# Padded rows of pieces and a new order of work at the layer ends of a four-layer graph network

## The chip, the cores and the metric

The kernel runs on one core of one Trainium2 chip. The metric is device time in microseconds (us), the median of several runs. TensorE (PE; its weight loads are PEld), VectorE (DVE), ScalarE (ACT), GpSimd (POOL) and SyncE (SP) have instruction streams of their own and meet through semaphores. SP and POOL also issue DMAs, in the order of their streams.

## What is computed

A graph of N = 3327 nodes with 512 features passes through four layers. `adj` is a dense 0/1 matrix. Layers 0, 1 and 2 are graph attention with 8, 4 and 8 heads, layer 3 is a mean over neighbours with dense weights:

```python
# layers 0, 1, 2  (layer 1 adds self loops to the mask)
h  = max(layernorm(x), 0)
Wh = h @ W                                   # per head
e  = leaky_relu(s1[i] + s2[j], slope 0.2)    # s1, s2: Wh times two vectors
x  = x + elu(softmax(where(adj, e, -inf)) @ Wh)
# layer 3
h  = max(layernorm(x), 0)
agg = (adj @ h) / max(degree, 1)
x  = x + max(concat(h @ W_self + b_self, agg @ W_nb + b_nb) @ W_comb + b_comb, 0)
```

## The kernel before, in words

Nodes are cut into 26 tiles of 128 (the last has 127). Targets go in 7 chunks of four tiles (the last has two, tiles 24 and 25); sources in five groups of 6, 6, 6, 4 and 4 tiles (`JG`, line 67).

**Attention without exponentials per edge.** exp(leaky_relu(s1 + s2)) is one product of node terms where s1 + s2 > 0 and another where it isn't. So for each head and source tile there is a gate (s1 > -s2, by ACT at L550 or DVE at L547), which is ANDed with the mask (L556) and, for the other half, XORed back (L560). Masks and gates are FP8 and are the stationary operand. The moving operand is the node's value terms for both cases. To keep f32 precision each is cut into three bf16 **pieces**: a head's row holds for each case (a "half") 3 x 65 = 195 columns in layers 0 and 2. L588 multiplies the first half with one gate, L591 the second half with the other. In layer 1 the heads are wider: L584 (3 x 129 = 387 bf16 columns) for group 0, and for the other groups f32 pairs (L581) with gates cast up by ACT or DVE (L493).

**Layout of a row** (`dims`, line 102): the first half takes `AO` = 196 columns (195 and a column of ones that gives the degree in layer 0), the row `HW` = 2 x 196 - 1 = 391 columns, 782 bytes. `pieces` (line 298) makes the rows of one tile and stores them to scratch memory `abd`; `load_pieces` (line 498) loads one group of one head, `nj` rows side by side in each partition, into a tile `ab` with seven buffers. Each pass takes two target tiles k; for each source j it runs L588 and L591 for the first k, then for the second. R (L606) sums the pieces.

**Node terms of the next layer, in hooks.** When a chunk is done, its tiles go through stages that `hooks.run` spreads among the passes that follow: s0 `finish` (load own terms `xt`, ELU on ACT and DVE, add on POOL at L664, store) and `norm` (statistics on DVE at L282 and L284, the power on POOL L285 to L287, ACT L289); s1 transposes on PE (L134) with a copy by ACT (L138); s2 projection on PE (L340; in layer 3 L377) and, in layers 0 to 2, the making and storing of pieces; s3 transposes and stores the row scores s1 (`send_s1`, L392 to L395), which the next layer loads as `s1b` (L518). The last chunk has nothing behind it, so its two tiles go through the stages after the layer's last products.

**The end of a layer** (lines 637 to 641): start the first of the last tiles, run what is `left` (in layer 2: own-term projections for layer 3 of the tiles from 22 on, L377 with a bias addition at L380), drain the hooks, then `close()`, then run what is left again. `close` calls `fuse_weights` in layers 0 and 1: it multiplies W_self or W_nb by its half of W_comb in four blocks: load (L170), transpose (L134 on `xt`), four products (L174), copy (L176), store (L177); and one row for the biases (L180, L181).

**Order.** The program is written in one order; a list scheduler then places instructions on their engines by priority, where `after(a, b)` asks that a stand behind b on its engine. `gone` holds the last product of each pass. Each engine then runs its stream strictly in order.

Of the kernel before, what the change touches and what calls it, by code (L numbers as in the profile page):

```python
# [37 lines left out]
P = 128  # L38
# [14 lines left out]
def tile_gnn(ctx: ExitStack, tc: tile.TileContext, x, adj, W0, a01, W1, al, ar, W2, a2,  # L53
# [41 lines left out]

    xs = [x] + [[dram.tile([n * P, D], F32, name=f"x{l}_{c}") for c, (_, n) in enumerate(chunks)]
# [5 lines left out]
    def dims(l):  # L102

        H = heads[l]
        DA = D // H + 1
        AO = 3 * DA + 1
        return H, DA, AO, (2 * AO - 1 if l != 1 else 2 * AO)
# [39 lines left out]
    gone = []  # L147

# [12 lines left out]
    def fuse_weights(i, wc):  # L161
        w_src, b_src = ((Ws, bs), (Wn, bn))[i]
        b = pre.tile([P, KC], F32, name="bv", bufs=1)
        if i == 0:
            nc.gpsimd.dma_start(bias, bc.partition_broadcast(P))
        with nc.allow_non_contiguous_dma(reason="512 values"):
            nc.gpsimd.dma_start(b, b_src.rearrange("(c p) -> p c", p=P))
        for k in range(KC):
            w = pre.tile([P, D], F32, name="xt")
            nc.gpsimd.dma_start(w, w_src[k * P:(k + 1) * P, :])  # L170
            wT = transposed(w, pre, "hT")
            pw = ps.tile([P, D], F32, name="mm")
            for m in range(KC):
                nc.tensor.matmul(pw, wT[:, m, :], wc[:, m, :], start=(m == 0), stop=(m == KC - 1))  # L174
            xo = pre.tile([P, D], F32, name="h")
            nc.scalar.copy(xo, pw)  # L176
            nc.gpsimd.dma_start(Xd[i][k * P:(k + 1) * P, :], xo)  # L177
        pb = ps.tile([P, D], F32, name="mm")
        for m in range(KC):
            nc.tensor.matmul(pb, b[:, m:m + 1].to_broadcast([P, P]), wc[:, m, :], start=(m == 0), stop=(m == KC - 1))  # L180
        nc.vector.tensor_add(bias, bias, pb)  # L181
# [54 lines left out]
    def open_layer(l):  # L236
        L = Layer()
        L.l = l
        if l == 3:
# [40 lines left out]
    def norm(xt, pool):  # L280
# [3 lines left out]
        nc.vector.bn_aggr(mv[:, 0:2], st)  # L284
# [13 lines left out]
    def pieces(L, t, AB, pool, first):  # L298
# [9 lines left out]
        nc.gpsimd.memset(pt[:, :, :, o, 3 * DA:AO] if l == 1 else pt[:, :, o, 3 * DA:AO], 1.0)  # L308
# [14 lines left out]
        if o == two - 1 and l == 1:  # L323
            for a in range(2):
                nc.sync.dma_start(abd[l][g][:, a, :, js, :].rearrange("h p j w -> p h j w"), pt[:, :, a])
        elif o == two - 1:
            stored[t] = nc.sync.dma_start(abd[l][g][:, :, js, :].rearrange("h p j w -> p h j w"), pt).ins.name

    def project(L, t, hT, pool, first):
# [7 lines left out]
        for f in range(2):  # L337
            pw = (accs if first else ps).tile([P, D // 2 + H], F32, name="acc" if first else "mm")
            for k in range(KC):
                nc.tensor.matmul(pw, hT[:, k, :], L.w[:, k, f, :], start=(k == 0), stop=(k == KC - 1))  # L340
# [13 lines left out]
        if l == 1 and KIND[g] != "b":  # L354
            for f in range(2):
# [5 lines left out]
                nc.sync.dma_start(abd[l][g][hs, :, :, jj, :].rearrange("h a p w -> p h a w"),  # L361
                                  pt.rearrange("p h a s d -> p h a (s d)").bitcast(F32))
# [7 lines left out]
    def project_last(L, t, hT, i):  # L370
# [5 lines left out]
        for k in range(KC):  # L376
            nc.tensor.matmul(pw, hT[:, k, :], L.w[i][:, k, :], start=(k == 0), stop=(k == KC - 1))  # L377
        if i == 0:
            y = pre.tile([P, D], F32, name="AB", bufs=1)
            nc.vector.tensor_add(y, pw, bias)  # L380
            nc.sync.dma_start(y1d[c][kk * P:kk * P + n, :], y[:n])
# [7 lines left out]
    def send_s1(L, t, pool, first):  # L389
# [5 lines left out]
        nc.sync.dma_start(s1d[L.l][:, t * P:(t + 1) * P], s1t[:H])  # L395

    def node_stages(L, t, get_x, pool, first=False):
# [7 lines left out]
        def s1():  # L405
            behind = gone[-1] if gone else None
            q["hT"] = transposed(q["h"], mp, "A", 6, behind) if late else transposed(q["h"], pool, "hT", 2, behind)
# [7 lines left out]
        def s3():  # L415
            if L.l != 3:
                send_s1(L, t, pool, first)
# [834 lines left out]
```

## Time and profile before

| | us |
|---|---|
| median of 3 runs | 3674.61 (3668.65 to 3675.11) |
| profiled execution | 3671.68 |
| its span, first to last instruction | 3669.8 |

Stages of the span, from windows of the trace:

| stage | from, to (us) | PE busy | DVE busy | ACT busy | granted PE clock | DMA share |
|---|---|---|---|---|---|---|
| first node terms | 0, 177 | 127.75 | 128.87 | 108.09 | 0.97 | 0.75 |
| layer 0 | 177, 1263 | 1065.72 | 896.78 | 850.46 | 0.99 | 0.73 |
| end of layer 0 | 1263, 1308 | 34.48 | 25.01 | 37.22 | 0.89 | 0.68 |
| layer 1 | 1308, 2156 | 816.41 | 717.92 | 680.43 | 0.99 | 0.78 |
| end of layer 1 | 2156, 2200 | 23.56 | 24.89 | 25.56 | 0.73 | 0.57 |
| layer 2 | 2200, 3309 | 1105.47 | 785.14 | 750.79 | 1.00 | 0.55 |
| end of layer 2 | 3309, 3356 | 37.54 | 10.96 | 10.98 | 0.89 | 0.72 |
| layer 3 | 3356, 3670 | 297.74 | 61.78 | 54.42 | 0.98 | 0.32 |

A busy time counts every moment in which some instruction of the engine is under way. PE's instructions overlap, so its busy time does not tell how fast one follows another; the start times do. The granted clock is the share of TensorE's full clock in the stretch. "Idle before, releaser" behind a group is the time its engine stood still just before it and what ended that.

### The profile page before, as it was taken

How to read it: one execution, taken by the hardware profiler on the slowest of the kernel's cores; microseconds unless marked ns; L12 is line 12 of the kernel's file. 1: busy time of each engine (PE TensorE's matmuls, PEld its weight loads, DVE VectorE, ACT ScalarE, POOL GpSimd, SP SyncE). 2: the span in 40 equal slices, each digit the busy share in tenths (PEclk: the TensorE clock that was granted, in tenths of full speed). 3: DMA queues.
4: the chain of work that ended last, by engine and by line, in shares of the span. 5: the costliest groups of instructions: out<-in, count | busy, mean ns of one | idle time of the engine just before them, and what ended most of it. 6: DMA issues, size and time to landing. Idle time of an engine off the chain costs nothing. (4 is left out here: it accounts for less than half of the span.)

```text
span 3669.8 us, 78902 instructions
## 1 busy us (share of the span) xinstructions
PE 3508.7 (96%) x31348; PEld 3172.0 (86%) x31348; DVE 2651.4 (72%) x5230; ACT 2518.0 (69%) x4170; POOL 589.2 (16%) x832
## 2 busy tenths in 40 slices
PE   7799999999999899999999979999999999998998
PEld 5599999999999778888888859989898989886886
DVE  7698888888887789888888766767776767672121
ACT  5678787777787779888888656767666767571111
POOL 6501221202010102122223220001010101010000
PEclk9999999999999999999999989999999999999999
DMA  7777677777756877777877876545455554476331
GB/s 210 230 207 226 201 226 212 215 220 224 220 189 215 270 262 262 270 257 249 275 249 261 320 229 188 187 169 189 167 182 167 191 171 171 160 276 238 113 104 51
DMA packets 321402, 773.05 MB, mean 211 GB/s; under 512 B 36037, under 2 KB 143560, under 8 KB 320384
## 3 DMA queue, kind: packets, MB, share of 16 engines
q1 hardware_dynamic: 293920, 707.23, 57.6%
q0 software_dynamic: 27104, 60.69, 6.8%
q8 instruction: 249, 4.08, 0.4%
q14 instruction: 129, 1.06, 0.1%
HBM read 661.25 MB, written 128.68 MB: 215 GB/s over the span
## 5 line engine op out<-in xcount | busy, mean ns | idle before, releaser
L588 PE MATMUL acc<-ab,tht 128*128 128x195 bf16 (+1 forms) x10816 | 1872.8, 248 | 20.9 <-DVE tht L556 14.5
L591 PE MATMUL acc<-ab,gt 128*128 128x195 bf16 (+1 forms) x10816 | 1872.3, 249 | 3.1 <-DVE gt L560 2.3
L550 ACT ACTIVATE gt<-s1b,ks 128x512 fp8e4<-128x512 f32 (+1 forms) x2464 | 1456.5, 677 | 279.0 <-issue 150.4
L588 PEld LDWEIGHTS <-tht 128*128 128x128 fp8e4 x10816 | 1060.0, 98 | 28.0 <-DVE tht L556 15.4
L591 PEld LDWEIGHTS <-gt 128*128 128x128 fp8e4 x10816 | 1052.6, 97 | 26.6 <-issue 14.6
L581 PE MATMUL acc<-ab,t 128*128 128x258 f32 x4160 | 544.6, 289 | 22.7 <-ACT t L493 19.6
L581 PEld LDWEIGHTS acc<-ab,t 128*128 128x128 f32 x4160 | 520.2, 192 | 35.8 <-ACT t L493 23.1
L556 DVE TENSOR_TENSOR tht<-gt,m 128x768 uint32<-128x768 uint32 (+3 forms) x560 | 447.8, 800 | 141.6 <-ACT gt L550 138.8
L560 DVE TENSOR_TENSOR gt<-tht,m 128x768 uint32<-128x768 uint32 (+3 forms) x560 | 447.0, 799 | 8.2
L493 ACT CAST t<-tht 128x1536 fp32r<-128x1536 fp8e4 x208 | 300.7, 1469 | 57.6 <-PE acc L581 47.2
L547 DVE TENSOR_SCALAR gt<-s1b,ns 128x512 fp8e4<-128x512 f32 (+1 forms) x448 | 213.9, 480 | 150.0 <-PE acc L591 138.3
L664 POOL TENSOR_TENSOR xt<-xt,e 128x512 f32<-128x512 f32 x78 | 114.7, 1471 | 1270.8 <-DVE e L663 1230.6
L788 PE MATMUL acc<-y,mf 128*128 128x512 f32 x1352 | 309.8, 391 | 1.3 <-DVE mf L783 1.3
L550 ACT ACTIVATE tht<-s1b,ks 128x512 fp8e4<-128x512 f32 (+1 forms) x504 | 306.9, 679 | 2.0 <-DMA s1b<-s 2.0
L788 PEld LDWEIGHTS acc<-y,mf 128*128 128x128 f32 x1352 | 253.6, 188 | 57.4 <-DVE mf L783 1.7
L606 DVE TENSOR_REDUCE R<-acc 128x130 f32<-128x390 f32 x416 | 214.7, 555 | 81.8 <-PE acc L591 81.7
L584 PE MATMUL acc<-ab,tht 128*128 128x387 bf16 x1248 | 225.5, 329 | 4.6 <-DMA ab<-ab 2.5
L785 ACT CAST mf<-m 128x768 fp32r<-128x768 fp8e4 (+1 forms) x78 | 59.1, 762 | 244.7 <-PE acc L788 232.9
L340 PE MATMUL mm<-w,hT 128*128 128x260 f32 (+1 forms) x832 | 200.3, 393 | 13.2 <-ACT hT L138 10.4
L340 PEld LDWEIGHTS mm<-w,hT 128*128 128x128 f32 x832 | 156.9, 194 | 38.4 <-ACT hT L138 11.2
L584 PEld LDWEIGHTS <-tht 128*128 128x128 fp8e4 x1248 | 118.7, 98 | 81.9 <-DMA ab<-ab 2.9
L319 POOL TENSOR_TENSOR pt<-r 128x520 bf16<-128x520 f32 (+1 forms) x116 | 143.2, 1254 | 266.1 <-DVE r L315 249.3
(132 smaller groups left out, 3138.2 us busy)
## 6 DMA issues: line engine op xcount, KB each, us to landing
ab<-ab SPq DMA_DIRECT2D x336, 586.5 KB
ab<-ab SPq DMA_DIRECT2D x224, 391.0 KB
ab<-ab SPq DMA_DIRECT2D x112, 774.0 KB
ab<-ab SPq DMA_DIRECT2D x112, 516.0 KB
ab<-ab SPq DMA_DIRECT2D x56, 582.0 KB
s1b<-s SPq DMA_DIRECT2D x120, 256.0 KB
m<-mask SPq DMA_DIRECT2D x72, 384.0 KB
ab<-pt SPq DMA_DIRECT2D x40, 516.0 KB
```

The lines of the kernel that those rows point to most:

```text
L340: nc.tensor.matmul(pw, hT[:, k, :], L.w[:, k, f, :], start=(k == 0), stop=(k == KC - 1))
L493: (nc.scalar.copy if KIND[g] == "s" else nc.vector.tensor_copy)(t[:, :k1 - k0, :nj], th[a][g][:, k0:k1])
L547: nc.vector.tensor_scalar(gv[:, :, jj, :], s1v, L.ns2[:, j, h:h + 1], 2.0, op0=ALU.is_gt, op1=ALU.mult, saturate=False)
L550: nc.scalar.activation(gv[:, :, jj, :], s1v, AF.Relu, bias=L.ks2[:, j, h:h + 1], scale=BIG, saturate=False)
L556: nc.vector.tensor_tensor(pu, gu, mu, ALU.bitwise_and)
L560: nc.vector.tensor_tensor(gu, pu, mu, ALU.bitwise_xor)
L581: mm = nc.tensor.matmul(acc[k][:, :2 * DA], thr[g][:, k - ks[0], jj, :], ab[a][g][:, jj, :], start=(j == 0), stop=(j == NT - 1), skip_grou ...
L584: mm = nc.tensor.matmul(acc[k][:, :3 * DA], th[a][g][:, k, jj, :], ab[a][g][:, jj, :3 * DA], start=(j == 0), stop=(j == NT - 1), skip_grou ...
L588: nc.tensor.matmul(acc[k][:, :3 * DA + o], th[0][g][:, k, jj, :], ab[0][g][:, jj, :3 * DA + o], start=(j == 0), stop=False, skip_group_che ...
L591: mm = nc.tensor.matmul(acc[k][:, AO - o:HW], th[1][g][:, k, jj, :], ab[0][g][:, jj, AO - o:HW], start=False, stop=(j == NT - 1), skip_gro ...
L606: nc.vector.tensor_reduce(R[:, k], v.rearrange("p a (s d) -> p a d s", s=3), AX.X, ALU.add)
L788: nc.tensor.matmul(acc[k], mf[:, jj, :], y2[g][:, jj, s, :], start=(j0 + jj == 0 and s == 0), stop=(j0 + jj == NT - 1 and s == 1))
```

## The change

It has four parts.

1. **Rows.** In layers 0 and 2 each half is rounded up to 200 columns and the row is 400 (800 bytes). The columns 195 to 199 of both halves are set to ones, and the degree is the sum of two columns. Layer 1's rows stay. The tile `ab` grows accordingly.
2. **Blocks of weights.** `fuse_weights` becomes the class `Fusion`: loads of biases and of blocks 0 and 1 are issued ahead of the last head, blocks 0 and 1 and the biases are run right behind the last products, and blocks 2 and 3 at the end. Own terms x of the last chunk's tiles are loaded ahead of the last head too, by POOL.
3. **End of layer 2.** The projections that are left are run behind the last products; their bias additions and stores are asked to stand behind the statistics of the last chunk's first tile.
4. **Queues.** Behind the first layer's own node terms, stores of pieces are held back to stage s3 (`to_store`), and row scores are stored by POOL instead of SP. The transposes of tile 25 stand behind the projection of tile 24. Buffers: "A" from 6, 5, 6 to 8, 6, 8 in the three layers, "tht" in layer 1 from 12 to 11, "R" in layer 2 smaller.

The core of the diff:

```diff
+    A_BUFS = [8, 6, 8]
...
         DA = D // H + 1
-        AO = 3 * DA + 1
-        return H, DA, AO, (2 * AO - 1 if l != 1 else 2 * AO)
+        AO = -(-(3 * DA + 1) // 8) * 8 if l != 1 else 3 * DA + 1
+        return H, DA, AO, 2 * AO
...
-        nc.gpsimd.memset(pt[:, :, :, o, 3 * DA:AO] if l == 1 else pt[:, :, o, 3 * DA:AO], 1.0)
+        nc.gpsimd.memset(pt[:, :, :, o, 3 * DA:AO] if l == 1 else
+                         pt[:, :, o].rearrange("p h (a w) -> p h a w", a=2)[..., 3 * DA:AO], 1.0)
...
+    class Fusion:
...
+        def load(self, k, behind):
+            self.w[k] = pre.tile([P, D], F32, name="xt")
+            after(nc.gpsimd.dma_start(self.w[k], self.w_src[k * P:(k + 1) * P, :]), behind)
+
+        def block(self, k, behind):
+            w = self.w.pop(k)
+            wT = transposed(w, pre, "hT", 2, behind)
             pw = ps.tile([P, D], F32, name="mm")
             for m in range(KC):
+                nc.tensor.matmul(pw, wT[:, m, :], self.wc[:, m, :], start=(m == 0), stop=(m == KC - 1))
+            nc.scalar.copy(w, pw)
+            nc.gpsimd.dma_start(Xd[self.i][k * P:(k + 1) * P, :], w)
...
+        def biases(self, behind):
+            pb = ps.tile([P, D], F32, name="mm")
+            for m in range(KC):
+                mm = nc.tensor.matmul(pb, self.b[:, m:m + 1].to_broadcast([P, P]), self.wc[:, m, :],
+                                      start=(m == 0), stop=(m == KC - 1))
+                if m == 0:
+                    after(mm, behind)
+            nc.vector.tensor_add(bias, bias, pb)
...
         if i == 0:
-            y = pre.tile([P, D], F32, name="AB", bufs=1)
-            nc.vector.tensor_add(y, pw, bias)
-            nc.sync.dma_start(y1d[c][kk * P:kk * P + n, :], y[:n])
+            def add():
+                y = pre.tile([P, D], F32, name="AB", bufs=1)
+                sm = nc.vector.tensor_add(y, pw, bias)
+                if behind:
+                    after(sm, stats[-chunks[-1][1]])
+                nc.sync.dma_start(y1d[c][kk * P:kk * P + n, :], y[:n])
+            if behind:
+                return add
+            add()
...
-        nc.sync.dma_start(s1d[L.l][:, t * P:(t + 1) * P], s1t[:H])
+        (nc.sync if first else nc.gpsimd).dma_start(s1d[L.l][:, t * P:(t + 1) * P], s1t[:H])
...
-            behind = gone[-1] if gone else None
+            behind = (L.mm if t == NT - 1 and not first else gone[-1]) if gone else None
...
         def s3():
             if L.l != 3:
+                for to, pt in L.to_store:
+                    nc.sync.dma_start(to, pt)
+                L.to_store = []
                 send_s1(L, t, pool, first)
             elif late:
-                left.append(lambda: project_last(L, t, q["hT"], 0))
+                left.append(lambda: project_last(L, t, q["hT"], 0, gone[-1]))
...
             for h in range(H):
+                if last and h == H - 1:
+                    for k in range(nt):
+                        x_last[t0 + k] = load_x(l, t0 + k, mp, "A", A_BUFS[l], behind=gone[-1])
+                    fusion = close()
+                    if fusion:
+                        fusion.load_biases()
+                        fusion.load(0, gone[-1])
+                        fusion.load(1, gone[-1])
...
-                                    mm = nc.tensor.matmul(acc[k][:, AO - o:HW], th[1][g][:, k, jj, :],
-                                                     ab[0][g][:, jj, AO - o:HW], start=False, stop=(j == NT - 1),
+                                    mm = nc.tensor.matmul(acc[k][:, AO:AO + 3 * DA + o], th[1][g][:, k, jj, :],
+                                                     ab[0][g][:, jj, AO:AO + 3 * DA + o], start=False, stop=(j == NT - 1),
...
-                                nc.vector.tensor_copy(deg2[:n, t0 + k:t0 + k + 1], acc[k][:n, 3 * DA:AO])
+                                nc.vector.tensor_reduce(deg2[:n, t0 + k:t0 + k + 1],
+                                                        acc[k][:n, 3 * DA:AO + 3 * DA + 1:AO], AX.X, ALU.add)
...
         hooks.run(1, 0, 0)
-        run_left()
+        fusion = close()
+        if fusion:
+            for k in range(2):
+                fusion.block(k, gone[-1])
+            fusion.biases(gone[-1])
+        adds = run_left()
         hooks.drain()
-        close()
-        run_left()
+        for add in adds:
+            add()
+        if fusion:
+            for k in range(2, KC):
+                fusion.load(k, gone[-1])
+                fusion.block(k, gone[-1])
+        for add in run_left():
+            add()
```

## The prediction

> **What bounds the kernel now.** First the busy times of the whole execution:
>
> ```profile
> PE 3508.7 (96%) x31348; PEld 3172.0 (86%) x31348; DVE 2651.4 (72%) x5230; ACT 2518.0 (69%) x4170; POOL 589.2 (16%) x832
> ```
>
> PE is busy 96% of the span, so next the costliest groups:
>
> ```profile
> L588 PE MATMUL acc<-ab,tht 128*128 128x195 bf16 (+1 forms) x10816 | 1872.8, 248 | 20.9 <-DVE tht L556 14.5
> L591 PE MATMUL acc<-ab,gt 128*128 128x195 bf16 (+1 forms) x10816 | 1872.3, 249 | 3.1 <-DVE gt L560 2.3
> ...
> L584 PE MATMUL acc<-ab,tht 128*128 128x387 bf16 x1248 | 225.5, 329 | 4.6 <-DMA ab<-ab 2.5
> ```
>
> 10816 + 10816 = 21632 products belong to layers 0 and 2, and they waited only 24 us in all. The 248 ns are a length in a pipeline, not a pace: in the list of instructions in order of time a product starts every 83 to 88 ns. Then a table by stage (columns: stretch, length, busy us and instructions of PE, PEld, DVE, ACT, POOL, granted clock, DMA share, GB/s):
>
> ```profile
> 177.00:1263.00 1086.00, 1065.72 (x11891) 1046.62 (x11892) 896.78 (x1825) 850.46 (x1510) 162.81 (x247) 0.99 0.73 219
> 1263.00:1308.00 45.00, 34.48 (x129) 20.85 (x127) 25.01 (x54) 37.22 (x65) 12.39 (x23) 0.89 0.68 236
> ...
> 2156.00:2200.00 44.00, 23.56 (x108) 16.79 (x107) 24.89 (x46) 25.56 (x48) 14.49 (x20) 0.73 0.57 177
> 2200.00:3309.00 1109.00, 1105.47 (x11275) 1005.58 (x11274) 785.14 (x1589) 750.79 (x1280) 83.61 (x124) 1.00 0.55 185
> 3309.00:3356.00 47.00, 37.54 (x113) 20.76 (x111) 10.96 (x26) 10.98 (x16) 7.84 (x13) 0.89 0.72 290
> ```
>
> Inside layers 0 and 2 PE is the bound (98% and 99.7% busy), so there the pace of a product is the time. At the three layer ends PE is not busy and its granted clock falls to 0.73 to 0.89. Last, PE in order of time at these ends (start, length, group, idle before and its releaser):
>
> ```profile
> 1272.98 1.11 PE L134 MATMUL tp<-ident,h 128*128 128x128 f32 x4 [9.42 <-ACT h L289]
> ...
> 1288.13 7.07 PE L174 MATMUL mm<-w,hT 128*128 128x512 f32 x16
> ...
> 1303.83 3.60 PE L180 MATMUL mm<-w,bv 128*128 128x512 f32 x8
> ```
>
> ```profile
> 2166.53 1.12 PE L134 MATMUL tp<-ident,h 128*128 128x128 f32 x4 [10.00 <-ACT h L289]
> 2177.37 6.89 PE L340 MATMUL mm<-w,hT 128*128 128x264 f32 x16 [9.73 <-ACT hT L138]
> ```
>
> ```profile
> 3323.35 1.12 PE L134 MATMUL tp<-ident,h 128*128 128x128 f32 x4 [6.90 <-ACT h L289]
> ```
>
> While PE waits for the layernorm of the last tiles, the block work (L134 on xt, L174, L180), which needs nothing of them, stands behind them.
>
> **Part 1, padded rows.** In a group's tile, row jj of pieces starts at 782 jj bytes and its second half 392 bytes later. From the start times in nanoseconds of 61 whole passes of layers 0 and 2 I averaged the step from each product to the next, by its row. Second-half products whose start is a multiple of 16 bytes (jj = 4): 83.4 and 83.4 ns for the two target tiles. At 8, 6, 4 and 14 bytes past one (jj = 0, 1, 2, 5): 86.7 to 88.1. First-half products for the first target tile: 83.9 at jj = 0 (a multiple), 86.6 to 88.3 at all others; for the second target tile 83.3 to 84.7 everywhere. The pattern is the same in all five groups, though groups of 4 and 6 rows place the weights differently, so it belongs to the row, not to the weight load. Mean of all: 85.62; mean of those that start on a multiple of 16: 83.50. After the change rows step 800 bytes and halves 400, so all starts are multiples of 16: 21632 x 2.12 ns = **45.9 us**.
>
> The open point is that second halves then start 16 bytes past a multiple of 32, which no row of 195 columns shows now. The nearest row is L584: its rows step 776 bytes, so jj = 2 starts 16 past a multiple of 32 and steps 163.2 and 163.6 ns, as fast as jj = 4 (163.4, on a multiple of 32), while jj = 1 and 3 (8 past 16) step 168.4 and 168.3 for the first target tile. I take 46. Upper end: every product at the fastest row's 83.3, 50 us. Lower end: second halves at the slowest row's 88.1 against 86.2 now, -20 us, and first halves from 85.0 to 83.5, +16: -4 us.
>
> The rule in the Trainium skill, "TensorE: Matmul & The Clock Gate", section "Wait — 56ns, not 53.3ns?", is that warm products start exactly N / 2.4 GHz + 2.5 ns apart, with no term for the address. For 195 columns that would be an estimated 83.75 ns wherever a row starts, padding would bring nothing, and the sum below would be 26 instead of 72 us. The trace's 83.5 on multiples of 16 agrees with it and the 85.6 over all does not, so the measurement decides.
>
> What padding adds: loads and stores of pieces grow by 9/391, 2.3%; the DMA share of 0.73 becomes 0.74 and PE waited for pieces 6.3 us at L588 in all, so I cost it at nothing (if the cover fails, those 6 us again). The memset L308 writes 80 instead of 8 elements; at L319's 1254 ns per 520 elements the other 72 cost at most 0.17 us, 52 times 9 us on a POOL that is 16% busy: nothing. L609 becomes a reduce, 26 times, bounded by 0 and L606's 555 ns: at most 11 us of DVE over 1086 us in which DVE has 189 idle: nothing.
>
> **Part 2, block work behind the last products (ends of layers 0 and 1).** Moved up: blocks 0 and 1 and the biases. Half of L174 (7.1 us), two block transposes (about 0.9) and L180 (3.6): 11.6 us of PE work. It needs its weights on chip: their loads move from behind the tail to before the last head. The end of layer 0 has 9.42 us idle, which this fills; the clock was at half from 1268.8 to 1279.1, in which 5.4 us of PE work ran, so 2.7 more if it stays up: 12.1. Its cost is four ACT copies (L138 572 ns, L176 578) among the layernorm's, 2.3 us, covered because 11.6 exceeds 9.4 by 2.2. What is late next is ACT: it then has to make the next layer's gates with 12 us less of PE delay, and in layer 1 it is 80% busy. I take 4 off: **8 us**. Layer 1's end has 19.7 us idle, so the 11.6 go in whole; I count **12**. Half of that gap is another wait:
>
> ```profile
> 2175.52 1.33 ACT L550 ACTIVATE gt<-s1b,ks 128x512 fp8e4<-128x512 f32 x2 [9.04 <-DMA s1b<-s]
> 2176.76 0.56 ACT L138 COPY hT<-tp 128x512 f32<-128x512 f32 x1
> ```
>
> The copy that PE needs stands on ACT behind gates that wait for the row scores, and no edit touches that. Bounds for both ends together: 0 (all refilled) to 12.1 + 11.6 + 3.7 (half of the 7.3 us that ran at half clock) + 7 = 34; the 7 is this wait of POOL for the own terms (behind L664: the statistics of the last tile and a weight load), which the early load removes:
>
> ```profile
> 2171.63 1.26 POOL L664 TENSOR_TENSOR xt<-xt,e 128x512 f32<-128x512 f32 x1 [6.00 <-DMA xt<-x]
> ```
>
> **Part 3, end of layer 2.** The layernorm of tile 24 stands on DVE behind a bias addition:
>
> ```profile
> 3319.26 0.69 DVE L380 TENSOR_TENSOR AB<-mm,bias 128x512 f32<-128x512 f32 x1 [4.92 <-DMA y<-AB]
> 3319.86 0.68 DVE L282 BATCH_NORM_STATS2 st<-xt 128x6 f32<-128x512 f32 x1
> ```
>
> Its input was ready at 3315.69 (end of L664), so 4.2 us go, since the change puts these additions behind the statistics. The next wait is the rest of that chain, 2.7 of the 6.9 us; with so short a gap part of the half clock (3320.2 to 3330.5, 6.4 us of work) goes too: 2. Sum **6**, between 0 and 4.5 + 3.2 = 8.
>
> **Part 4, queues.** 52 stores of row scores and six loads of own terms go from SP to POOL (about 0.6 us each as L665: 35 us in 2000). Behind a waiting store on POOL stand the next tile's L319 and L285 to L287, which wait for DVE anyway (L319: 249 us). On SP they leave, and stores of pieces come one step later, behind loads already issued; two buffers hold them and PE waits for neither. Nothing, between -5 and +5. The skill's "SBUF — State Buffer", section "SBUF: two separate sides", warns that POOL-issued DMAs starve behind some DVE work; the trace lands such stores (L665) in a median 5.1 us, and nothing early needs these. "A" buffers 5 to 6 and "tht" 12 to 11 in layer 1: nothing, see the rivals.
>
> **Sum.** 46 + 8 + 12 + 6 = 72. The profiled execution took 3671.7 (span 3669.8): 3599.7. The median of the runs is 2.9 above it, so I predict **3602 us**. A measurement of this kernel tells about 0.2% (7.3 us) from no change.
>
> **Rivals.**
> 1. Rows gain, ends refill (0.23): ACT's gates, not PE, end the first head of the next layer. For it: ACT is busy 37.2 of 45 us in 1263 to 1308. Against: PE there works off 11 us of blocks that ACT doesn't need. Only the 46 stay: 3674.6 - 46 = 3628.
> 2. The padding doesn't do what it says (0.10): second halves at 16 past 32 stay slow; 0 for rows, 26 for ends: 3648. Against: L584, jj = 2.
> 3. More than forecast (0.11): PE's idle times at chunk starts of layer 1 (2.2, 3.2, 3.4, 3.5, 3.4 us, each with the clock at half after it) go with the sixth "A": 16 us and some 4 of clock: 3582. Against: they end with ACT's cast L493, and ACT had not paused.
> 4. Slower (0.04): "tht" 11 instead of 12 holds ACT back by one group per head in layer 1, six gates of 0.68 us, 4.1 us in 28 heads: +115, 3717. It decides from (72 + 7) / 28 = 2.8 us a head. Against: ACT idles 168 us there, 6 a head, and two heads need only 10.
>
> Forecast 0.48; the remaining 0.04 is within 0.2% by small losses that eat the ends. So faster 0.92, same 0.04, slower 0.04. Range 3580 to 3640: it holds the forecast, rival 1 and most of rival 3, and leaves out rival 2, 4 and the rest, 0.18, and the tail of 3.
>
> **What would show it.** Steps of L588 and L591 near 83.5 ns for every row, with L584's unchanged; blocks (L174's work) in the 9.4 and 10.0 us gaps with the clock at full; no bias addition ahead of L282 at the end of layer 2. Wrong if second halves still step 87 ns, if idle time before the first products of layers 1 and 2 grows by what left the ends, or if layer 1 (848 us from 1308 to 2156) gets longer.

## The result, and the profile after

| | before | after |
|---|---|---|
| median in us, runs side by side | 3671.63 (4 runs, 3668.56 to 3675.11) | 3628.16 (4 runs, 3622.15 to 3630.75) |
| ratio, 95% interval | | 0.9879, 0.9863 to 0.9895 |
| span of the profiled execution | 3669.8 | 3627.9 |

The kernel became 43.5 us faster; 72 were forecast. The time lies inside the range (3580 to 3640), 26 us above the predicted 3602. It falls on the number of rival 1, but not for rival 1's reason, as will be seen.

First I cut both traces at the same events instead of at fixed times. A layer runs from its closing-terms product (layer 0: from its first piece product) to its last piece product; an end is what lies between that and the next layer's closing terms (end 2: up to the first product of layer 3). The windows of the kernel after, in the order layer 0, end 0, layer 1, end 1, layer 2, end 2 (columns: stretch, length, busy us and instructions of PE, PEld, DVE, ACT, POOL, granted clock, DMA share, GB/s):

```profile
172.50:1249.20 1076.70, 1052.96 (x11893) 1032.56 (x11894) 895.73 (x1824) 850.44 (x1510) 177.88 (x276) 0.99 0.74 224
1249.20:1314.10 64.90, 60.30 (x327) 43.83 (x324) 42.85 (x86) 54.13 (x83) 12.86 (x24) 0.95 0.71 250
1314.10:2149.20 835.10, 793.57 (x5691) 694.38 (x5691) 692.78 (x1304) 663.03 (x922) 203.49 (x240) 0.98 0.75 267
2149.20:2207.30 58.10, 50.99 (x339) 37.90 (x337) 39.73 (x70) 44.92 (x80) 15.92 (x23) 0.94 0.64 227
2207.30:3272.70 1065.40, 1062.70 (x11045) 969.22 (x11046) 769.07 (x1564) 731.22 (x1248) 84.59 (x124) 1.00 0.56 189
3272.70:3300.40 27.70, 23.69 (x59) 10.40 (x57) 9.42 (x23) 9.31 (x14) 8.06 (x13) 0.94 0.84 339
```

The same stages of all kernels of this study, in us, with the kernel before on top:

| kernel | median | first node terms | layer 0 | end 0 | layer 1 | end 1 | layer 2 | end 2 |
|---|---|---|---|---|---|---|---|---|
| before | 3671.6 | 176.9 | 1086.3 | 69.0 | 824.0 | 73.7 | 1079.4 | 33.3 |
| **after** | 3628.2 | 172.5 | 1076.7 | 64.9 | **835.1** | 58.1 | 1065.4 | 27.8 |
| rows_only | 3638.5 | 173.3 | 1080.6 | 68.7 | 819.5 | 69.8 | 1066.7 | 33.2 |
| rows_392 | 3640.2 | 174.0 | 1080.1 | 64.5 | 833.8 | 58.0 | 1074.3 | 27.7 |
| ends_back | 3653.5 | 172.2 | 1077.9 | 78.5 | 834.8 | 72.7 | 1063.5 | 26.1 |
| x_late | 3637.3 | 171.0 | 1080.7 | 63.9 | 834.0 | 62.6 | 1066.5 | 27.8 |
| adds_back | 3630.4 | 172.3 | 1074.6 | 64.9 | 834.5 | 58.1 | 1065.4 | 34.1 |
| queues | 3626.6 | 170.7 | 1074.1 | 63.9 | 832.9 | 57.8 | 1064.3 | 28.7 |
| l1_a5 | 3622.5 | 170.1 | 1073.6 | 64.6 | 833.7 | 57.6 | 1063.4 | 28.7 |
| **l1_bufs** | **3611.2** | 174.2 | 1071.1 | 62.4 | 820.8 | 58.1 | 1065.1 | 27.7 |
| l1_t13 | 3611.8 | 171.9 | 1073.9 | 64.7 | 823.2 | 57.4 | 1063.9 | 26.1 |
| both | 3615.8 | 171.7 | 1077.7 | 64.0 | 824.7 | 57.9 | 1064.8 | 28.7 |

After against before: first node terms -4.4, layer 0 -9.6, end 0 -4.1, layer 1 **+11.1**, end 1 -15.6, layer 2 -14.0, end 2 -5.5, layer 3 +0.2; sum -41.9, the difference of the spans. Six kernels (after, ends_back, adds_back, l1_a5, l1_bufs, l1_t13) have the same passes in layer 0, and it lasts 1071.1 to 1077.9 us in them: one profile tells that stage to some 3 us either way. Layer 2 agrees to 2 us.

Between end 0 and layer 1 the product of the closing terms is no even cut: it stands behind 208 products of layer 1 in the kernel before and in rows_only, behind 223 in all others. Cut at the 200th product of layer 1 instead, end 0 holds 302 instructions of PE in both kernels. Before:

```profile
1263.20:1331.00 67.80, 57.20 (x302) 41.18 (x301) 45.74 (x93) 58.88 (x92) 12.90 (x23) 0.92 0.64 220
1331.00:2156.20 825.20, 793.69 (x5716) 694.31 (x5715) 697.19 (x1300) 658.77 (x913) 192.23 (x211) 0.99 0.79 270
```

and after:

```profile
1249.20:1309.80 60.60, 56.61 (x302) 41.12 (x300) 39.43 (x79) 49.84 (x77) 12.86 (x24) 0.94 0.70 244
1309.80:2149.20 839.40, 797.27 (x5718) 697.09 (x5716) 696.21 (x1311) 667.33 (x928) 203.49 (x240) 0.98 0.75 268
```

So for equal work end 0 gained 7.2 us, not 4.1, and layer 1 lost **14.2**, not 11.1; in l1_bufs layer 1 takes 824.8 us by this cut, as before.

The groups of products after:

```profile
L631 PE MATMUL acc<-ab,tht 128*128 128x195 bf16 (+1 forms) x10816 | 1845.3, 248 | 14.9 <-DVE tht L599 12.0
L634 PE MATMUL acc<-ab,gt 128*128 128x195 bf16 (+1 forms) x10816 | 1844.8, 248 | 10.5 <-ACT gt L593 6.1
```

L631 and L634 are the former L588 and L591; L627 is the former L584. The mean of one is still 248 ns, since that is a length in the pipeline; it is the busy time of the two groups that fell. From start to start the steps are now 84.17 ns (85.63 before) for every row, either half and either target tile (row by row 84.1 to 84.2). The unchanged L627 steps 165.3 (165.2 before).

Ends 0 and 1 after, PE in order of time:

```profile
1250.72 7.13 PE L181 MATMUL mm<-w,hT 128*128 128x512 f32 x16
...
1265.60 6.26 PE L362 MATMUL mm<-w,hT 128*128 128x260 f32 x16 [3.88 <-ACT hT L141]
```

```profile
2150.58 7.13 PE L181 MATMUL mm<-w,hT 128*128 128x512 f32 x16 [0.24 <-ACT hT L141]
...
2167.24 6.06 PE L362 MATMUL mm<-w,hT 128*128 128x264 f32 x16 [5.66 <-ACT hT L141]
```

The blocks (L181, the former L174) and right behind them the biases (L195, 3.60 us) stand where PE was idle for 9.42 and 10.00 us, and those idle times are gone. What is left is one wait each for the copy of a transposed tile.

The stage that got worse is layer 1. Its waits before (stretch 1333 to 2140; columns: engine and line, what was waited for, us in total, times, longest):

```profile
PE acc L581 <- ACT t L493: 17.8, 9, 3.5
ACT t L493 <- DVE tht L615: 9.8, 7, 4.5
DVE tht L556 <- ACT tht L550: 6.9, 8, 1.7
```

and after (L624, L527, L659, L599 and L593 are the former L581, L493, L615, L556 and L550; L599 ANDs a gate with the mask):

```profile
DVE tht L599 <- ACT tht L593: 41.7, 23, 4.2
ACT t L527 <- DVE tht L659: 29.9, 19, 4.4
PE acc L624 <- ACT t L527: 29.4, 13, 4.4
```

DVE waits for ACT's gates, ACT's casts for DVE's flips, PE for the casts. PE's idle time in layer 1 rose from 31.5 to 41.5 us: 10 of the 14.2 us lost.

### The profile page after: what moved, and what is told of

It reads as the page before. It is cut to its first block, busy times and chain, and to the rows that moved or that the text cites. A ratio compares the mean times of both kernels' runs of the same rounds, so it can differ in the third digit from the quotient of the medians.

```text
span 3627.9 us, 78882 instructions
## 1 busy us (share of the span) xinstructions
PE 3479.3 (96%) x31348; PEld 3143.1 (87%) x31348; DVE 2642.1 (73%) x5227; ACT 2517.0 (69%) x4170; POOL 620.6 (17%) x893
## 3 DMA queue, kind: packets, MB, share of 16 engines
q1 hardware_dynamic: 292480, 713.17, 57.8%
## 5 line engine op out<-in xcount | busy, mean ns | idle before, releaser
L631 PE MATMUL acc<-ab,tht 128*128 128x195 bf16 (+1 forms) x10816 | 1845.3, 248 | 14.9 <-DVE tht L599 12.0
L634 PE MATMUL acc<-ab,gt 128*128 128x195 bf16 (+1 forms) x10816 | 1844.8, 248 | 10.5 <-ACT gt L593 6.1
L593 ACT ACTIVATE gt<-s1b,ks 128x512 fp8e4<-128x512 f32 (+1 forms) x2464 | 1456.3, 677 | 250.2 <-issue 144.3
L634 PEld LDWEIGHTS <-gt 128*128 128x128 fp8e4 x10816 | 1061.2, 98 | 32.2 <-issue 16.1
L631 PEld LDWEIGHTS <-tht 128*128 128x128 fp8e4 x10816 | 1061.5, 98 | 25.4 <-DVE tht L599 13.3
L624 PE MATMUL acc<-ab,t 128*128 128x258 f32 x4160 | 547.5, 290 | 33.3 <-ACT t L527 29.4
L624 PEld LDWEIGHTS acc<-ab,t 128*128 128x128 f32 x4160 | 522.8, 193 | 47.1 <-ACT t L527 34.2
L599 DVE TENSOR_TENSOR tht<-gt,m 128x768 uint32<-128x768 uint32 (+3 forms) x560 | 447.2, 799 | 143.3 <-ACT gt L593 140.6
L527 ACT CAST t<-tht 128x1536 fp32r<-128x1536 fp8e4 x208 | 300.0, 1468 | 60.1 <-DVE tht L659 29.9
L593 ACT ACTIVATE tht<-s1b,ks 128x512 fp8e4<-128x512 f32 (+1 forms) x504 | 306.8, 679 | 1.8 <-DMA s1b<-s 1.8
L854 PEld LDWEIGHTS acc<-y,mf 128*128 128x128 f32 x1352 | 253.6, 188 | 57.6 <-DVE mf L849 1.9
L627 PE MATMUL acc<-ab,tht 128*128 128x387 bf16 x1248 | 225.2, 329 | 3.9 <-DMA ab<-ab 2.2
L627 PEld LDWEIGHTS <-tht 128*128 128x128 fp8e4 x1248 | 118.4, 98 | 80.7 <-DMA ab<-ab 2.2
```

The lines of the kernel that those rows point to most:

```text
L527: (nc.scalar.copy if KIND[g] == "s" else nc.vector.tensor_copy)(t[:, :k1 - k0, :nj], th[a][g][:, k0:k1])
L593: nc.scalar.activation(gv[:, :, jj, :], s1v, AF.Relu, bias=L.ks2[:, j, h:h + 1], scale=BIG, saturate=False)
L599: nc.vector.tensor_tensor(pu, gu, mu, ALU.bitwise_and)
L624: mm = nc.tensor.matmul(acc[k][:, :2 * DA], thr[g][:, k - ks[0], jj, :], ab[a][g][:, jj, :], start=(j == 0), stop=(j == NT - 1), skip_grou ...
L627: mm = nc.tensor.matmul(acc[k][:, :3 * DA], th[a][g][:, k, jj, :], ab[a][g][:, jj, :3 * DA], start=(j == 0), stop=(j == NT - 1), skip_grou ...
L631: nc.tensor.matmul(acc[k][:, :3 * DA + o], th[0][g][:, k, jj, :], ab[0][g][:, jj, :3 * DA + o], start=(j == 0), stop=False, skip_group_che ...
```

## The experiments

Each was timed beside the kernel before; "expected" is what was on record before it ran.

### What the rows give by themselves: rows_only

The kernel before with part 1 alone:

```diff
-        AO = 3 * DA + 1
-        return H, DA, AO, (2 * AO - 1 if l != 1 else 2 * AO)
+        AO = -(-(3 * DA + 1) // 8) * 8 if l != 1 else 3 * DA + 1
+        return H, DA, AO, 2 * AO
```

> The kernel before with nothing but the padded rows (row 400, halves 200, memset, degree as a sum of two columns). Theory: the rows alone take the step of a product from 85.63 to 84.2 ns, 21632 x 1.45 = 31 us, and touch nothing else: 3672 - 31 = 3641, layer 1 (from the product of its closing terms to its last product) stays at 824 us, ends stay at 69, 74 and 33. Rival: the whole gain of 43 us is the rows' and all else cancels by chance: 3628 to 3632.

Measured: 3638.51, ratio 0.9911 (0.9895 to 0.9926); steps 84.17 ns. Layer 2 is 12.7 us shorter than before, layer 0 only 5.7, with PE idle 28.8 us in it instead of 20.3; ends 0 and 2 are as before, end 1 is 3.9 us shorter, layer 1 4.5. Its 32.1 us (the kernel before, beside it: 3670.65) are about three quarters of the whole gain. That they meet the 31 expected is partly luck: of 31.3 us in the spans only 18.4 lie in layers 0 and 2, and 12.0 in the first node terms (3.6), end 1 and layer 1, which the theory left untouched; why is not shown. Rival 1 (only the rows gain) also falls, as the kernel after is 10 us faster than the rows alone although it loses in layer 1.

### Whether a multiple of 16 bytes is what matters: rows_392

The kernel after with rows of 784 bytes. First halves start on a multiple of 16, second halves 8 past one.

```diff
-        AO = -(-(3 * DA + 1) // 8) * 8 if l != 1 else 3 * DA + 1
+        AO = 3 * DA + 1
```

> The changed kernel with rows of 392 columns (784 bytes, a multiple of 16) and second halves at 196 columns (392 bytes, 8 past a multiple of 16). Theory that multiples of 16 bytes matter: first halves step about 84, second halves 87 to 88 as in row 0 before, mean 85.5, so 21632 x 1.3 = 28 us of the rows' gain are gone: 3656. Rival that a multiple of 4 or 8 bytes is enough, since only odd multiples of 2 were cured: 84.2 everywhere, 3628.

Measured: 3640.22, ratio 0.9914 (0.9899 to 0.9929), 12 us above the kernel after. Steps 85.08: second halves 86.7 to 87.1, but first halves 83.3 to 83.5, below the 84.17 that they take when all are aligned. The place matters, but less than expected (0.91 ns a product, 20 us in 21632 products, instead of 28; the time shows 12 of them): a slow product makes the next one step less than an aligned one does among its like.

### The pace of products alone: products

TensorE runs series of 320 products of 195 columns (the last three of 387) with nothing else at work; only the start of the columns differs.

```python
def series(name, src, dst, count=320, cols=195):
    acc = accs.tile([P, 512], F32, name="acc")
    for i in range(count):
        a, b = src[i % len(src)], dst[i % len(dst)]
        nc.tensor.matmul(acc[:, b:b + cols], gates[:, i % 8, :], rows[:, a:a + cols], ...)
```

> Nothing of the network is computed; the output is zeros. TensorE alone runs series of 320 products of 128x128 FP8 weights with 195 bf16 columns, which differ in where the columns start (0, 2, 4, 6, 8, 12, 14, 16 and 32 bytes past a multiple of 32), then alternations of two or four starts and places in PSUM, and 387 columns at 0, 8 and 16. No other engine touches the memory meanwhile. Theory: the start address sets the pace, so a series steps 84.0 to 84.3 ns at 0, 16 and 32 bytes and 86.5 to 88.5 at all others, 2 to 4 ns apart, and 387 columns 163.5 to 165 at 0 and 16 and 168 at 8; an alternation of a multiple of 16 with one 8 past it steps 85 on average, the slow one 86.7 and the fast one 83.4. The place in PSUM (784 or 800 bytes) changes nothing. Rival 1: the pace is that of N columns at the clock with a constant, and the slow rows in the kernel came from other engines or DMAs that touched the same memory: 84 at every start. Rival 2: it is the place in PSUM: alternations with second halves at 784 bytes step slower than at 800 at equal starts.

Measured, mean step in ns from the start times:

| starts, bytes past a multiple of 32 | step |
|---|---|
| all 0; all 4; all 8; all 16; all 32 | 84.17 |
| all 2; all 6 | 85.00 |
| all 12; all 14 | 85.83 |
| 0 and 400 in turn (to PSUM at 784 or 800 bytes); 0 and 416 in turn; 8 and 408 in turn | 84.17 |
| 0 and 392 in turn, to PSUM at 784 or at 800 bytes | 85.00 (84 and 86 in turn) |
| 0, 0, 392, 392 in turn | 84.58 |
| 387 columns, all 0; all 8; all 16 | 164.17 |

In windows of 24 us from the middle of the series at 0, 12 and 0/392 (the count of PE's instructions includes some three that reach over an edge):

```profile
22.00:46.00 24.00, 24.00 (x288) 24.00 (x286) 0.00 (x0) 0.00 (x0) 1.00 0.01 1
...
158.00:182.00 24.00, 24.00 (x282) 24.00 (x281) 0.00 (x0) 0.00 (x0) 1.00 0.01 1
320.00:344.00 24.00, 24.00 (x285) 24.00 (x283) 0.00 (x0) 0.00 (x0) 1.00 0.00 1
```

At full clock in all three, 288, 282 and 285 products. The place in PSUM has no part, and no other engine is needed to slow a product: both of those rivals fall. My own rule falls as well in its simple form. Starts 8 past a multiple of 16 are as fast as aligned ones so long as all products start there (84.17); they cost when they alternate with aligned ones (85.00).

### The two kernels' own sequences: products_seq

```python
def passes(row, half, count=6):
    return [(k, row * jj + h * half, h * half) for nj in (6, 6, 6, 4, 4)
            for jj in range(nj) for k in range(2) for h in range(2)] * count
```

> Nothing of the network is computed; the output is zeros. TensorE alone again, two accumulators. First 193 to 198 columns from one aligned start. By the steps of the run before (84.17 for 195 columns, 164.17 for 387), which are what an even number of columns one higher would take at 2.4 columns per ns and 2.5 ns more, I expect 83.33, 83.33, 84.17, 84.17, 85.00 and 85.00; rival: even steps of 0.42 per column. Then the starts of the two kernels in the order in which they use them, 26 rows for two target tiles. Theory, that starts alone make the difference between the kernels: rows of 782 bytes with halves at 392 step 85.5 to 85.7 on average, as the kernel before does (85.62), with second halves slower than first; rows of 784 with halves at 392 step 85.0 to 85.1; rows of 800 with halves at 400 step 84.17. Rival: other engines and DMAs have a part: then 782 steps less than 85.2 here. Last, runs of eight products from one start and eight from another: if a change of the start's place within 16 bytes costs, and not the place itself, 0 against 8 bytes is all 84.17 but for one slow step of some 86 at one of the two changes, and 0 against 16 has none.

Measured: 193 and 194 columns 83.33, 195 and 196 84.17, 197 and 198 85.00. Rows of 782 bytes with halves at 392: **85.58** (85.62 in the kernel before). Rows of 784: 85.00 (85.08 in rows_392). Rows of 800: **84.17** (84.17 in the kernel after). Windows of 52 us from the three:

```profile
144.00:196.00 52.00, 52.00 (x610) 52.00 (x609) 0.00 (x0) 0.00 (x0) 1.00 0.00 1
197.00:249.00 52.00, 52.00 (x615) 52.00 (x613) 0.00 (x0) 0.00 (x0) 1.00 0.00 1
250.00:302.00 52.00, 52.00 (x620) 52.00 (x619) 0.02 (x1) 0.00 (x0) 1.00 0.01 2
```

The pattern by row comes back too: in the 782-byte rows, jj = 0 steps 84.0, 87.8, 83.4, 86.6 (kernel before: 83.9, 88.1, 83.3, 86.9), jj = 4 steps 88.0, 83.7, 83.3, 83.0. So the sequence of start addresses alone makes the whole difference of pace between the two kernels. Eight products from 0 and then eight from 8 bytes: the first from 8 steps 86.7, the next three 83.3, mean 84.17. The change back to 0 costs nothing, and neither do changes between 0 and 4, 16 or 400 bytes or between 8 and 24. So a delay is made good by the next products, if they have room; in turn with every product (0 and 392) there is too little.

### Whether the blocks fill the ends: ends_back

The kernel after, with blocks 0 and 1 and the biases behind the drained hooks again; all early loads stay.

```diff
-        if fusion:
-            for k in range(2):
-                fusion.block(k, gone[-1])
-            fusion.biases(gone[-1])
         adds = run_left()
         hooks.drain()
...
-            for k in range(2, KC):
-                fusion.load(k, gone[-1])
-                fusion.block(k, gone[-1])
+            for k in range(KC):
+                if k > 1:
+                    fusion.load(k, gone[-1])
+                fusion.block(k, N_.mm)
+            fusion.biases(N_.mm)
```

> The changed kernel with blocks 0 and 1 and the biases put back behind the drained hooks at the ends of layers 0 and 1; their early loads and the early loads of own terms stay. Theory: the 11.6 us of PE work in the gaps is what shortened the ends, so PE's idle time at these ends goes back from 4.6 and 7.1 us to about 9 and 19, the end of layer 0 gets 4 us longer and that of layer 1 11 to 12 us (58 to about 70, not to 73.7, since the own terms still come early): 3643 us, 3638 to 3647. Rival: the early own terms did it, and the blocks fill only time that the next wait would take: ends within 2 us of the changed kernel's, 3626 to 3631 us.

Measured: 3653.54, ratio 0.9958 (0.9944 to 0.9971), 25 us above the kernel after: end 0 +13.6, end 1 +14.6. PE in order of time:

```profile
1259.89 1.11 PE L137 MATMUL tp<-ident,h 128*128 128x128 f32 x4 [9.42 <-ACT h L308]
...
1290.98 0.91 PE L137 MATMUL tp<-ident,xt 128*128 128x128 f32 x4 [4.87 <-DMA xt<-in_L_gnn_W_self_dram]
...
2173.71 1.12 PE L137 MATMUL tp<-ident,h 128*128 128x128 f32 x4 [10.00 <-ACT h L308]
```

The idle times of 9.42 and 10.00 us are back to the hundredth, so the blocks were what filled them. The direction is settled, the size is more than the 15 expected, because this kernel adds a wait that neither of the two has: the weights of block 2 go into a buffer that block 0 frees only now, and PE waits for them 4.87 us here and 6.20 us in end 1. Without these 11 us some 17 (28.2 - 11) are left for the move.

### What the early own terms give: x_late

```diff
-                        x_last[t0 + k] = load_x(l, t0 + k, mp, "A", A_BUFS[l], behind=gone[-1])
+                        x_last[t0 + k] = lambda t=t0 + k: load_x(l, t, mp, "A", A_BUFS[l])
...
-        xt = x_last.pop(t) if t in x_last else load_x(l, t, pre, "xt", 2)
+        xt = x_last.pop(t)() if t in x_last else load_x(l, t, pre, "xt", 2)
```

> The changed kernel, but the own terms of the last chunk's two tiles are loaded when these tiles are finished, by SP as before, and not ahead of the last head by POOL (still into the same buffers, so no other buffer is shared anew). Theory: the early load removed a wait of its own, beside the blocks: the addition of the last tile at the end of layer 1 waits for its own terms again, some 6 us as in the kernel before (6.00), the layernorm of that tile and all behind it with it: the end of layer 1 goes from 58.1 to 62 to 64 us, the ends of layers 0 and 2 by 0 to 6 us, the time from 3628 to 3633 to 3642 us. Rival: the wait returns but lies beside the block work that PE now does there: ends within 2 us of the changed kernel's, 3625 to 3631 us.

Measured: 3637.25, ratio 0.9899 (0.9883 to 0.9916). End 1 is 62.6 instead of 58.1; ends 0 and 2 don't move. First POOL's addition, then PE's projection behind it:

```profile
2164.37 1.26 POOL L730 TENSOR_TENSOR A<-A,e 128x512 f32<-128x512 f32 x1 [5.39 <-DMA A<-x]
```

```profile
2171.71 6.56 PE L362 MATMUL mm<-w,hT 128*128 128x264 f32 x16 [9.72 <-ACT hT L141]
```

POOL's wait for the own terms returns (5.39; 6.00 before), and PE's second gap grows from 5.66 to 9.72, its old size (9.73). So the early load is worth 4.1 us at end 1, and PE's second gap there hung on it. Of the 9 us in the time only these 4.5 are placed; layer 0, which this edit does not reach until its last head, is 4.0 us longer in this profile (1080.7, where the six kernels above lie between 1071.1 and 1077.9), and the cause is open. ends_back shows the same from the other side: with the own terms early and the blocks late PE's second gap in end 1 is 0.68 us.

### Whether DVE's order shortened end 2: adds_back

```diff
-                if behind:
-                    after(sm, stats[-chunks[-1][1]])
...
-        adds = run_left()
-        hooks.drain()
-        for add in adds:
+        for add in run_left():
             add()
+        hooks.drain()
```

> The changed kernel with the bias additions of the projections that are left at the end of layer 2 right behind each projection, as before, and no longer behind the statistics. Theory: the addition stands ahead of the statistics on DVE again and the end of layer 2 goes from 27.8 back to 32 or 33 us: 3632 to 3633 us. Rival: it was the place of the projections on PE, or the early own terms, that shortened this end: 27 to 29 us, 3626 to 3629 us.

Measured: end 2 34.1 instead of 27.8 us, with PE's gap before the transposes 7.68 instead of 2.72. The whole, 3630.39, ratio 0.9889 (0.9873 to 0.9905), can't be told from the kernel after. DVE in this kernel:

```profile
3280.50 0.69 DVE L406 TENSOR_TENSOR AB<-mm,bias 128x512 f32<-128x512 f32 x1 [5.71 <-DMA y<-AB]
3281.10 0.68 DVE L301 BATCH_NORM_STATS2 st<-A 128x6 f32<-128x512 f32 x1
```

and in the kernel after:

```profile
3278.75 0.69 DVE L301 BATCH_NORM_STATS2 st<-A 128x6 f32<-128x512 f32 x1 [1.38 <-POOL A L730]
```

The kernel after leaves the 2.72 us that the prediction had named as the next wait (2.7). In adds_back, behind an addition that waits 5.71 us for the store of its only buffer stand the statistics that PE's last tile needs. The stage shows the theory right; the place of the projections is not what mattered.

### Where layer 1 loses: queues, l1_bufs, l1_a5, l1_t13, both

Queues back to the former order (the kernel after; row scores stored by SP, pieces stored at once):

```diff
-                L.to_store.append((abd[l][g][:, :, js, :].rearrange("h p j w -> p h j w"), pt))
+                nc.sync.dma_start(abd[l][g][:, :, js, :].rearrange("h p j w -> p h j w"), pt)
...
-        (nc.sync if first else nc.gpsimd).dma_start(s1d[L.l][:, t * P:(t + 1) * P], s1t[:H])
+        nc.sync.dma_start(s1d[L.l][:, t * P:(t + 1) * P], s1t[:H])
```

> The changed kernel with the stores as they were: row scores by SP, pieces stored as soon as they are made. Theory of the buffers: layer 1 stays at 835, time 3628 within 4. Rival of the queues: layer 1 back to 824, time 3617.

Measured: 3626.55, ratio 0.9884 (0.9869 to 0.9899); layer 1 stays at 832.9. The queues cost and give nothing that can be told, as forecast.

Both buffer counts of layer 1 back (l1_bufs):

```diff
-    A_BUFS = [8, 6, 8]
+    A_BUFS = [8, 5, 8]
...
-                    pt = mp.tile([P, PER * JM * P], FP8, name="tht", bufs=11 if l == 1 else 7)
+                    pt = mp.tile([P, PER * JM * P], FP8, name="tht", bufs=12 if l == 1 else 7)
```

> The changed kernel with layer 1's buffers as they were: 'A' 5, 'tht' 12. Theory: the 11 us that layer 1 lost (824 to 835) come from the eleventh instead of twelfth 'tht' buffer: layer 1 back to 824, time 3617. Rival (stores by POOL and later stores of pieces hold layer 1 up) and third (gates late because the end before it is shorter): 835 stays, time 3628.

Measured: **3611.22**, ratio 0.9841 (0.9828 to 0.9855), the best of the study and 17 us below the kernel after. Layer 1 is 820.8 against 835.1 after (both with 223 products ahead of the cut), PE idle 30.8 us in it (41.5 after, 31.5 before). The buffers are the cause; which of the two? l1_a5 takes the first line of that diff alone:

> The changed kernel with five instead of six buffers of A in layer 1, and eleven buffers of tht left as they are. Theory: the sixth A does the harm. With it DVE gets the four writes into A at a chunk's start done ahead of the flips of tht, ACT's casts wait for these flips, and PE for the casts; the new stalls come once per chunk and not once per head, as A does. Then layer 1 goes back from 835 to 819 to 823 us and the time is 3611 to 3616 us. Rival: one tht fewer does it (less room for ACT and DVE to run ahead): then layer 1 stays at 831 to 837 us and the time at 3624 to 3630 us. If both have a share, layer 1 lies between, near 828.

Measured: 3622.45, ratio 0.9876 (0.986 to 0.9891); layer 1 833.7. My theory fell: it is not the sixth "A". Layer 1's waits with five "A" and eleven "tht":

```profile
DVE tht L599 <- ACT tht L593: 41.3, 23, 4.2
ACT t L527 <- DVE tht L659: 30.0, 19, 4.4
```

and with five "A" and twelve "tht" (l1_bufs):

```profile
DVE tht L599 <- ACT tht L593: 10.3, 9, 2.9
ACT t L527 <- DVE tht L659: 4.1, 5, 1.3
```

So at five "A" the twelfth "tht" takes away most of both waits, and PE's idle time falls by the 10 us that the change had added. A head of layer 1 takes five, one for each group, flipped in place. Twelve thus hold two heads and two groups of a third, eleven one group of it. One more on top, thirteen, with four "A" in exchange (l1_t13):

> The changed kernel with thirteen tht and four A in layer 1. Theory: the number of tht is what lets ACT and DVE run ahead of PE there, 11 to 12 gave 12.7 us, so 13 gives more, at a falling rate: layer 1 at 810 to 817 us (from 820.8 with twelve), time 3600 to 3608 us. Rival: twelve cover one head and the start of the next, and what is left are the casts' other wait, for the products (28 us of ACT's idle time at twelve): 819 to 823 us, time 3609 to 3614 us. If four A hold the finish of a chunk back, layer 1 is longer than 823.

Measured: 3611.81, ratio 0.9839 (0.9826 to 0.9852), layer 1 823.2: the theory falls. The stage lies at the edge between the rival (819 to 823) and four "A" holding a chunk back (longer than 823), which this run can't tell apart: thirteen "tht" with four "A" give nothing over twelve with five; thirteen with five "A" were not run.

Last, l1_bufs with the queues as before (both):

> The changed kernel with twelve tht and five A in layer 1, and with the row scores stored by SynE's queue and the pieces stored at once, as before. Theory: the two edits add, 16.9 us of the one and 1.6 (within its uncertainty) of the other: 3608 to 3612 us. Rival: with layer 1's stall gone the queues begin to matter: apart from 3611 by more than 5 us.

Measured: 3615.83 (3610.44 to 3621.69), ratio 0.984 (0.9826 to 0.9853): above the 3608 to 3612 expected, but by the ratio the same as l1_bufs (0.9841). The 1.6 us of the queues were nothing.

## Why the prediction came out as it did

Forecast terms and what the traces gave: rows 46 against 23.6 (layers 0 and 2); ends 26 against 28.3 (7.2, 15.6 and 5.5; end 0 and layer 1 cut at the 200th product); layer 1 nothing against -14.2; first node terms nothing against 4.4; layer 3 nothing against -0.2. 72 against 41.9. Of the signs of being wrong that the prediction names one came true: layer 1 got longer.

**Part 1, right in mechanism, mis-sized.** The step that failed is "mean of those that start on a multiple of 16: 83.50". These products were no sample of aligned ones among their like: they stood behind products of 87 ns and made up for them. All aligned, a product steps 84.17, so the term is 21632 x (85.63 - 84.17) = 31.6 us instead of 45.9. Had I looked at pairs instead of single steps the error would have shown: at jj = 0 the first half is on a multiple of 16, yet its step depends on the target tile (83.9 and 83.3), that is, on what ran before it; and for the second target tile first halves were fast from every start (83.3 to 84.7). The list also left out jj = 3, whose second halves start 2 bytes past a multiple of 16 and yet step 83.6 and 84.7 (188 whole passes of the kernel before). Of the 31.6, layer 2 gave 14.0 of its 15.8. Layer 0 gave 9.6 in this profile, 11.7 on the mean of the six kernels with the same passes there (1074.6): PE idles 3.4 us more, and two more stretches of 3.4 us at half clock took 1.7 each. Faster products seem to meet ACT sooner: the waits of the second halves for its gates went from 0.7 to 6.1 us (L593), and rows_only, with nothing else changed, idles 28.8 us in layer 0. "The open point", halves 16 bytes past a multiple of 32, is settled: 84.17 like all others.

The rule that warm products start N / 2.4 GHz + about 2.5 ns apart (the Trainium skill, "TensorE: Matmul & The Clock Gate", "Wait — 56ns, not 53.3ns?") has no term for the start, and the runs show one: 84.17 to 85.83 ns for the same 195 columns. For aligned columns it is closer (83.75) than my 83.50: worked out with 196 columns it is an estimated 84.17, and with 388 columns 164.17, which are the measured 84.17 and 164.17 for 195 and 387. The pairs 193/194, 195/196 and 197/198 show that odd counts cost as much as the next even one.

**Part 2, right at end 0, too low at end 1.** For equal work end 0 gave 7.2 where I said 8. Its wait of 9.42 us is gone, and 3.88 us came back as a wait for ACT's copy (L141), close to the 4 that I had taken off for a refill by ACT, though I had thought of gates and not of a copy. End 1 gave 15.6 where I said 12: the blocks took the whole 10.00, and the second gap went from 9.73 to 5.66. That gap I had called untouched by any edit ("stands on ACT behind gates that wait for the row scores"). x_late shows otherwise: it returns with the late own terms (9.72). 10.0 + 4.1 = 14.1 of the 15.6. I had named POOL's wait of 6 us, but put it into the upper bound only.

**Part 3, right.** 6 forecast, 5.5 measured, 6.3 by adds_back; by DVE's order, as said.

**Part 4, the step "buffers nothing" failed.** Queues: nothing, as said. "tht" 12 to 11 cost 14 us in layer 1 (839.4 against 825.2 before and 824.8 in l1_bufs, cut at the 200th product). Rival 4 had this mechanism and its place, with a price of 4.1 us a head; measured are 0.5 (14 us in 28 heads); that ACT's idle time covers the rest is likely, but not shown. I had set it against the net sum, as a case that makes the kernel slower or does nothing, and left out the case between. I had argued that "two heads need only 10". What counts is what lies beyond the two heads, and there the buffer was one of two.

**Rivals.** 1 named the time (3628) and is wrong, so its number is luck: the rows did not give 46, and the ends kept their 28 us. 2 fell with 84.17 for every half. 3 fell: the stalls at chunk starts in layer 1 are still there after the change (2.95 to 4.38 us, 2.22 to 3.46 before), and five or six "A" make no difference.

What stays open: the 4.4 us of the first node terms (rows_only has 3.6 of them, the other kernels 2.7 to 6.8; nothing was tried on that); the 12.0 us of rows_only outside layers 0 and 2; 4.5 of the 9 us of x_late; and why a start at 2 or 6 bytes costs 0.83 ns and 0/392 in turn as much.

## What to carry to other kernels

A pace read off single steps of a pipeline is biased when a short step makes up for a long one: average over whole periods, or run the sequence by itself. Padding moving rows so that all starts are multiples of 16 bytes gave 1.7% per product here, for 2.3% more traffic of pieces, for which PE did not wait longer (1.8 us at L631, 6.3 at L588 before). Count buffers beyond what the rounds under way take, not out of the total: here one of the two spare ones was given away, which cost 17 us of the 60 that the same kernel gains with twelve (3611 us, the version to keep).

## What the runs showed of the hardware

- The start of the moving columns sets TensorE's pace: 195 bf16 columns step 84.17 ns from 0, 4, 8, 16 or 32 bytes past a multiple of 32, 85.00 from 2 or 6, 85.83 from 12 or 14, at full clock and with nothing else at work.
- The start before counts too: 0 and 392 bytes (8 past a multiple of 16) in turn step 85.00, though starts of either kind alone take 84.17. A single change from 0 to 8 costs one step of 86.7, which three steps of 83.3 make good; the change back, and changes between 0 and 4, 16 or 400 or between 8 and 24, cost nothing.
- Columns count in pairs: 193 to 198 columns step 83.33, 83.33, 84.17, 84.17, 85.00, 85.00.
- The place in PSUM (784 or 800 bytes) has no part in it.
